# Self products of 4096 rows on one core: which queue loads which part of the input, when, and in what packets

## Chip, cores and metric

One core of one Trainium2 chip. The metric is the device time of one execution in microseconds (us). The kernel before takes 1261.74 us, the median of three runs that lie between 1261.66 and 1261.79.

## What is computed

The input has 4096 rows of 256 float32 values. For each row all products of two of its values are wanted, the upper triangle only, row by row of the triangle: 32,896 products for each input row.

```python
def _L0_rec_ref(inputs):              # inputs: (4096, 256) float32
    dot = jnp.einsum('bi,bj->bij', inputs, inputs)
    iu, ju = jnp.triu_indices(inputs.shape[1])
    return dot[:, iu, ju]             # (4096, 32896) float32
```

The input is 4.19 MB, the output 538.97 MB.

## The kernel before

**Tiles.** Partition p holds the 32 input rows 32p to 32p+31, one after the other, in the tile `xt` (`flat` is the same tile as one long row a partition). Two rows make a *unit*: 512 floats, 2 KB a partition, 256 KB in all partitions. There are 16 units. The output of a unit is cut into three *pieces* of some 10,944 columns (`even_borders`), so there are 48 pieces. A piece is computed into one of two places in SBUF (`places`, `PLACES = 2`) and stored from there by one DMA (`sync`, line 392). A store moves, for each of 128 partitions, two contiguous runs of 43,776 or 44,032 bytes.

**Loop.** A *pass* `h` covers two units, that is six pieces `p` = 0 to 5 (`PASS = 6`). There are eight passes. The loop is rotated: pieces 0 and 1 of pass 0 are computed ahead (`AHEAD = 2`), and each turn of the hardware loop computes pieces 2 to 5 of pass `h` and then 0 and 1 of pass `h+1`. The very first piece is stored in five parts (`FIRST`), so that the first store can go out early; ScalarE (`scalar`) helps VectorE (`vector`) with the two pieces ahead.

**Who computes.** VectorE multiplies a stretch of a row by one broadcast value (line 275), GpSimd does the same for the tail of each piece (line 360). A piece's first VectorE instruction waits until the place is free (semaphore `free`, set by the store that last used it) and lets GpSimd start (`go`); VectorE's last instruction of the piece waits for GpSimd (`g_done`), and then SyncE issues the store (`v_done`).

**How the input comes in.** Three groups of loads:

- `NEAR`, issued by SyncE at the beginning (line 432): unit 0 alone; units 3, 4, 7 and 8 in runs of 4 KB; unit 12. That is six units.
- `EARLY`, issued by GpSimd at the beginning (line 327, called from the loop over `STEPS`): units 1, 2, 5 and 6 in runs of 4 KB. The 128 partitions are taken as a comb: every third partition in each of three DMAs (42 partitions each), and the last two partitions in a fourth.
- `LATE`, issued by GpSimd in pass 2 after piece 2 (`late`, line 327): units 9 to 11 and 13 to 15, in runs of 6 KB, as DMAs of 100, 3 and 25 partitions.

**Marks.** Between these DMAs GpSimd issues small ones (`mark`, line 321) that load two runs of 256 bytes a partition into a tile nobody reads, for a chosen number of partitions (`STEPS` = 5, 2, 2, 12, 4 and `SKIP` = 13).

**What waits for loads.** VectorE and ScalarE wait for unit 0 (`loaded[0]`) before they begin, GpSimd waits for it before its first `EARLY` load. Before the loop, VectorE and GpSimd wait for all `NEAR` loads, for `EARLY` (`far`) and for the marks. GpSimd waits for the `LATE` loads in pass 2 after piece 5.

**Queues.** Loads and stores that SyncE issues follow each other on its queue (q1). GpSimd's are on another queue (q0). Both are served by the same 16 DMA engines.

The first part of the first piece is computed by VectorE at line 236, in instructions that take both rows of the unit at once.

Of the kernel before, what the change touches and what calls it, by code (L numbers as in the profile page):

```python
# [12 lines left out]
P = 128  # L13
UNIT = 64
REPEAT = 2
PIECES = 3
EDGE = 32
NEAR = [(0, 1, 1), (3, 7, 2), (12, 13, 1)]
EARLY = (1, 5, 2)
LATE = (9, 13, 3)  # L20
WHEN = 2
BEGUN, HAD = 2, 5
HELPED = 1
HELP = 18.0
COMB = 3
STEPS = (5, 2, 2, 12, 4)
TENS, ODD, SKIP = 100, 3, 13
MARK = 64
PLACES = 2
SETS = 5  # L30
# [1 line left out]
AHEAD = 2  # L32
# [103 lines left out]
def kernel(  # L136
# [45 lines left out]
    loaded = [semaphore(f"loaded{k}") for k in range(len(NEAR))]  # L182
    far, marked = semaphore("far"), semaphore("marked")
    teeth = P // COMB
    rest = P - COMB * teeth

    def take(engine, sem, value: int):
        engine.wait_ge(sem, value).then_inc(sem, -value)  # L188
# [36 lines left out]
    def vector(h, pieces: range, ahead: bool, done: int = 0, joined: int = 0) -> tuple:  # L225
        for p in pieces:
            place, copied = places[p % PLACES], None
            parts = blocks(p, ahead)
            if ahead and p == 0:
                for c, (_, _, _, block, lo) in enumerate(parts):  # L230
                    if c == DIRECT:
                        nc.vector.tensor_copy(xp, x_of(h, 0)).then_inc(v_own, 1)  # L232
                        done += 1
                        copied = done
                    for i, j, at, length in block:
                        ins = nc.vector.tensor_tensor(  # L236
                            place[:, :, at - lo : at - lo + length],
                            window(x_of(h, 0)[:, j:], [[d, REPEAT], [1, 1], [1, length]]),
                            window(xp[:, i:] if c >= DIRECT else x_of(h, 0)[:, i:], [[d, REPEAT], [1, 1], [0, length]]),
                            ALU.mult,  # L240
                        )
                        if copied:
                            ins._wait_ge(v_own, copied).then_inc(go, 1)
                            copied = None
                    ins.then_inc(v_done, 1)
                continue
            shared = not ahead or p == HELPED
            if ahead and p == HELPED:
                take(nc.vector, x_copied, 1)
            first = None  # L250
            if not ahead and p % PIECES == 0:
                ins = nc.vector.tensor_copy(xv[:, :each], x_of(h, p // PIECES))  # L252
                ins._wait_ge(v_own, done).then_inc(v_done, 1)
                nc.vector.tensor_copy(xp, x_of(h, p // PIECES)).then_inc(v_own, 1)  # L254
                done += 1
                first = (v_own, done)
            if not ahead:
                if use(p) == uses:
                    take(nc.vector, free[p % PLACES], 16 * uses)
                elif first:  # L260
                    nc.vector.wait_ge(free[p % PLACES], 16 * use(p))  # L261
                else:
                    first = (free[p % PLACES], 16 * use(p))
            for _, _, _, block, lo in parts:
                order = interleave(block)
                waits = schedule(order)
                end = len(order) - 1
                if shared and end in waits:
                    waits[end - 1] = waits.pop(end)
                counted = {*waits.values(), *([end] if (p + 1) % PIECES == 0 else [])}  # L270
                number = {k: done + 1 + c for c, k in enumerate(sorted(counted))}
                assert 0 < min(counted, default=end) and end - 1 not in counted | {0}
                for k, ((i, j, at, length), m, _) in enumerate(order):
                    at -= lo
                    ins = nc.vector.tensor_tensor(  # L275
                        place[:, :, at : at + m * length],
                        window(xv[:, j:], [[d, REPEAT], [1, m], [1, length]]),
                        window(xp[:, i:], [[d, REPEAT], [1, m], [0, length]]),
                        ALU.mult,
                    )  # L280
                    if k == 0 and first:
                        ins._wait_ge(*first)
                    elif k == end and shared:
                        joined += 1
                        ins._wait_ge(g_done, joined)
                    elif k in waits:
                        ins._wait_ge(v_own, number[waits[k]])
                    if k in counted:
                        ins.then_inc(v_own, 1)
                    elif k == end:  # L290
                        ins.then_inc(v_done, 1)
                    elif k == 0 and not ahead:
                        ins.then_inc(go, 1)
                done += len(counted)
        return done, joined

    def scalar(pieces: range):

        xa = xt[:, 0, :each]
        for p in pieces:  # L300
            for _, _, block, _, lo in blocks(p, True):
                todo = [
                    nc.scalar.activation(  # L303
                        places[p][:, r, at - lo : at - lo + length],
# [4 lines left out]
                    for i, j, at, length in block  # L309
                    for r in range(REPEAT)  # L310
                ]
                if todo:
                    todo[-1].then_inc(a_done, 1)
                else:
# [5 lines left out]
        of = window(x_in[lo:hi], [[2 * MARK, 2], [1, MARK]])  # L320
        nc.gpsimd.dma_start(marks[lo:hi, :, :MARK], of).then_inc(marked, 16)  # L321

    def load(of_units: tuple, rows: slice):
        one, two, units = of_units
        dims = [[(two - one) * each, 2], [1, units * each]]
        to, of = (window(ap[rows, one * each :], dims) for ap in (flat, x_in))
        nc.gpsimd.dma_start(to, of).then_inc(far, 16)  # L327

    def late(h, p: int):
        with nc.gpsimd.If(h == WHEN):  # L330
            if p == BEGUN:
                load(LATE, slice(0, TENS))
                load(LATE, slice(TENS, TENS + ODD))
                mark(0, SKIP)
                load(LATE, slice(TENS + ODD, P))
            else:
                nc.gpsimd.wait_ge(far, 16 * (COMB + 4))
                nc.gpsimd.wait_ge(marked, 16 * (COMB + 3))
                nc.gpsimd.drain()

    def gpsimd(h, pieces: range, ahead: bool):

        done = turns = 0
# [6 lines left out]
        for p in [HELPED] if ahead else pieces:  # L350
            place = places[p % PLACES]
            block, lo = helped(p) if ahead else next((block, lo) for _, _, block, _, lo in blocks(p, False))
            turns += not ahead
            order = interleave(block)
            waits = schedule(order)
            counted = {*waits.values()}
# [14 lines left out]
                    ins.then_inc(g_own, 1)  # L371
            done += len(counted)
            ins.then_inc(g_done, 1)
            if p in (BEGUN, HAD) and not ahead:
                late(h, p)
        nc.gpsimd.sem_inc(g_own, -done)
        if turns:
            nc.gpsimd.sem_inc(go, -turns)  # L378

    def sync():  # L380
        done = ahead_done = 0
# [13 lines left out]
        for sem, count in ((v_done, done), (a_done, ahead_done)):  # L395
            nc.sync.sem_inc(sem, -count)

    def settle(counts: tuple):
        for sem, count in zip((v_own, g_done), counts):
            nc.vector.sem_inc(sem, -count)  # L400

    def all_pieces(engine, pieces_of):
        by_vector = engine is nc.vector
        counts = pieces_of(0, range(AHEAD), True)
        if by_vector:
            settle(counts)
        for sem in loaded[1:]:
            engine.wait_ge(sem, 16)
        engine.wait_ge(far, 16 * (COMB + 1))
        engine.wait_ge(marked, 16 * (COMB + 2))  # L410
        kind = engine.engine
        with nc.Fori(  # L412
            0,
# [4 lines left out]
            counts = pieces_of(h, range(AHEAD, PASS), False)  # L418
            with engine.If(h < passes - 1):
                nxt = nc.s_assert_within(h + 1, 0, passes - 1)  # L420
                if by_vector:
                    settle(vector(nxt, range(AHEAD), False, *counts))
                else:
                    pieces_of(nxt, range(AHEAD), False)
        if by_vector:
            nc.vector.wait_ge(v_own, counts[0]).then_inc(v_done, 1)
            settle(counts)

    for (one, two, units), sem in zip(NEAR, loaded):
        dims = [[(two - one) * each, 2 if two - one > units else 1], [1, units * each]]  # L430
        to, of = (window(ap[:, one * each :], dims) for ap in (flat, x_in))
        nc.sync.dma_start(to, of).then_inc(sem, 16)
    nc.vector.memset(edge, 0.0).then_inc(warm, 1)  # L433
    take(nc.scalar, warm, 1)
    nc.scalar.activation(edge[:, :1], edge[:, 1:2], AF.Copy, scale=edge[:, 2:3])  # L435
    for engine in (nc.vector, nc.scalar):
        engine.wait_ge(loaded[0], 16)
    at = 0
    for k, step in enumerate(STEPS):
# [44 lines left out]
```

## Time and profile before

| | |
|---|---|
| runs, median (lowest to highest) | 1261.74 us (1261.66 to 1261.79) |
| the profiled execution | 1261.66 us |
| span of its instructions | 1259.9 us |
| VectorE busy | 792.5 us, 63% of the span |
| GpSimd busy | 800.1 us, 64% |
| ScalarE busy | 27.1 us, 2% |
| bytes read / written in HBM | 4.21 MB / 538.97 MB |
| SyncE's loads at the beginning | issued from 0.96 us on, three |
| GpSimd's loads at the beginning | four, from 3.92 us on, with five marks, the last issued at 8.05 us |
| GpSimd's loads in pass 2 | three and a mark, issued from 364.40 to 366.39 us |

Times in the trace are counted from the first instruction of the span. The span leaves out what lies before the first and after the last instruction, here 1.8 us of the execution's time. "Issue to landing" of a DMA counts from the instruction on the issuing engine to the last of its completions, the time in the queue included. A DMA engine works through *packets*: one contiguous run, with its own size and time in the trace.

### The profile page before, as it was taken

How to read it: one execution, taken by the hardware profiler on the slowest of the kernel's cores; microseconds unless marked ns; L12 is line 12 of the kernel's file. 1: busy time of each engine (PE TensorE's matmuls, PEld its weight loads, DVE VectorE, ACT ScalarE, POOL GpSimd, SP SyncE). 2: the span in 40 equal slices, each digit the busy share in tenths (PEclk: the TensorE clock that was granted, in tenths of full speed). 3: DMA queues.
4: the chain of work that ended last, by engine and by line, in shares of the span. 5: the costliest groups of instructions: out<-in, count | busy, mean ns of one | idle time of the engine just before them, and what ended most of it. 6: DMA issues, size and time to landing. Idle time of an engine off the chain costs nothing. (4 is left out here: it accounts for less than half of the span.)

```text
span 1259.9 us, 2787 instructions
## 1 busy us (share of the span) xinstructions
DVE 792.5 (63%) x1256; ACT 27.1 (2%) x74; POOL 800.1 (64%) x1124
## 2 busy tenths in 40 slices
DVE  8656746667475674766647666486655866468560
ACT  8000000000000000000000000000000000000000
POOL 7477674776666766477665775567656676566750
DMA  9999999999999999999999999999999999999999
GB/s 375 441 427 441 429 437 431 434 434 434 436 433 428 435 435 431 435 428 438 430 438 430 439 428 438 430 438 431 434 436 431 437 431 436 429 436 429 440 428 395
DMA packets 15847, 543.25 MB, mean 431 GB/s; under 512 B 1466, under 2 KB 1504, under 8 KB 3296
## 3 DMA queue, kind: packets, MB, share of 16 engines
q1 hardware_dynamic: 14704, 540.54, 99.3%
q0 software_dynamic: 1136, 2.64, 0.6%
q14 instruction: 7, 0.06, 0.0%
HBM read 4.21 MB, written 538.97 MB: 431 GB/s over the span
## 5 line engine op out<-in xcount | busy, mean ns | idle before, releaser
L360 POOL TENSOR_TENSOR o<-xv 128x696 f32<-128x696 f32 (+33 forms) x1105 | 791.1, 756 | 416.8 <-DVE o L275 416.5
L275 DVE TENSOR_TENSOR o<-xv,xp 128x588 f32<-128x588 f32 (+4 forms) x1195 | 761.1, 712 | 430.3 <-DMA out_dram<-o 195.3
L303 ACT ACTIVATE o<-x 128x198 f32<-128x198 f32 (+34 forms) x72 | 25.5, 447 | 0.8 <-DMA x<-in_r_inputs_dram 0.8
L254 DVE COPY xp<-x 128x512 f32 x15 | 10.3, 688 | 0.0
L236 DVE TENSOR_TENSOR o<-x,xp 128x470 f32<-128x470 f32 (+18 forms) x19 | 9.7, 585 | 0.0
L236 DVE TENSOR_TENSOR o<-x 128x510 f32<-128x510 f32 (+9 forms) x10 | 5.7, 646 | 2.5 <-DMA x<-in_r_inputs_dram 2.5
L252 DVE COPY xv<-x 128x512 f32 x15 | 6.4, 427 | 0.5
L327 POOL DMA_DIRECT2D x<-in_r_inputs_dram x7 | 4.5, 649 | 1.6 <-DMA x<-in_r_inputs_dram 1.6
L321 POOL DMA_DIRECT2D marks<-in_r_inputs_dram x6 | 3.6, 602 | 1.2 <-SPq L175 1.2
L346 POOL MEMSET xv<- 128x1 f32 x1 | 0.1, 93 | 2.1 <-POOLq L188 2.1
L435 ACT ACT_TABLE_LOAD x1 | 1.3, 1283 | 1.2 <-ACTq L188 1.2
L433 DVE MEMSET edge<- 128x32 f32 x1 | 0.1, 85 | 1.0 <-SPq L175 1.0
L232 DVE COPY xp<-x 128x512 f32<-128x512 f32 x1 | 0.7, 684 | 0.0
L347 POOL COPY xv<-x 128x512 f32<-128x512 f32 x1 | 0.6, 609 | 0.0
L435 ACT ACTIVATE edge<-edge 128x1 f32<-128x1 f32 x1 | 0.3, 296 | 0.0
L471 POOL MEMSET const-float32-0.0<- 128x1 f32 x1 | 0.1, 98 | 0.2 <-issue 0.2
L471 POOL MEMSET const-bfloat16-1.0<- 128x1 bf16 x1 | 0.1, 101 | 0.0
L471 POOL MEMSET const-uint8-127<- 128x1 uint8 x1 | 0.1, 101 | 0.0
L471 POOL MEMSET const-float32-1.0<- 128x1 f32 x1 | 0.1, 98 | 0.0
## 6 DMA issues: line engine op xcount, KB each, us to landing
out_dram<-o SPq DMA_DIRECT2D x31, 10944.0 KB, 32.9
out_dram<-o SPq DMA_DIRECT2D x16, 11008.0 KB, 31.2
out_dram<-o SPq DMA_DIRECT2D x1, 4352.0 KB, 18.6
out_dram<-o SPq DMA_DIRECT2D x1, 2624.0 KB, 13.8
out_dram<-o SPq DMA_DIRECT2D x1, 1984.0 KB, 11.8
out_dram<-o SPq DMA_DIRECT2D x1, 1280.0 KB, 9.9
x<-in_r_inputs_dram POOLq DMA_DIRECT2D x1, 1200.0 KB, 39.7
x<-in_r_inputs_dram SPq DMA_DIRECT2D x1, 1024.0 KB, 5.2
```

What stands on the lines that cost most here:

```text
L232: nc.vector.tensor_copy(xp, x_of(h, 0)).then_inc(v_own, 1)
L236: ins = nc.vector.tensor_tensor(place[:, :, at - lo : at - lo + length], window(x_of(h, 0)[:, j:], [[d, REPEAT], [1, 1], [1, length]]), wi ...
L252: ins = nc.vector.tensor_copy(xv[:, :each], x_of(h, p // PIECES))
L254: nc.vector.tensor_copy(xp, x_of(h, p // PIECES)).then_inc(v_own, 1)
L275: ins = nc.vector.tensor_tensor(place[:, :, at : at + m * length], window(xv[:, j:], [[d, REPEAT], [1, m], [1, length]]), window(xp[:, i:] ...
L303: nc.scalar.activation(places[p][:, r, at - lo : at - lo + length], xa[:, r * d + j : r * d + j + length], AF.Copy, scale=xa[:, r * d + i ...
L321: nc.gpsimd.dma_start(marks[lo:hi, :, :MARK], of).then_inc(marked, 16)
L327: nc.gpsimd.dma_start(to, of).then_inc(far, 16)
L347: nc.gpsimd.tensor_copy(xv[:, :each], x_of(0, 0)).then_inc(g_own, 1)
L360: ins = nc.gpsimd.tensor_tensor(place[:, :, at : at + m * length], window(xv[:, j:], [[d, REPEAT], [1, m], [1, length]]), window(xv[:, i:] ...
L435: nc.scalar.activation(edge[:, :1], edge[:, 1:2], AF.Copy, scale=edge[:, 2:3])
L471: nc = _bacc.Bacc("TRN2", target_bir_lowering=False, num_devices=1)
```

## The change

SyncE's first load is split into the two rows of unit 0 (two DMAs in runs of 1 KB), and it then loads units 1, 2, 4 and 5 in runs of 4 KB and units 3 and 15 in runs of 2 KB: seven units. GpSimd loads nothing at the beginning; the comb and its marks are gone. In pass 1, ahead of piece 5, it loads units 6, 10 and 14 in runs of 2 KB and units 7 to 9 and 11 to 13 in runs of 6 KB: each group as one DMA of 120 partitions and one of 8, with a mark ahead of each of the four DMAs (5, 2, 7 and 3 partitions). It waits for them in pass 2, ahead of piece 5. The first instruction of the first part is done row by row: on VectorE as two instructions, on ScalarE by sorting the rows, with row 1's waiting for `loaded[1]`. GpSimd waits for both rows before it begins. The wait for `far` and `marked` ahead of the loop is gone. GpSimd's counts are now carried from the loop's pieces 2 to 5 into 0 and 1, as VectorE's were, and subtracted once (`settle`).

```diff
-NEAR = [(0, 1, 1), (3, 7, 2), (12, 13, 1)]
-EARLY = (1, 5, 2)
-LATE = (9, 13, 3)
-WHEN = 2
-BEGUN, HAD = 2, 5
+NEAR = [(1, 2, 3, 2), (3, 2, 12, 1)]
+LATE = [(6, 3, 4, 1), (7, 2, 4, 3)]
+BEGUN, HAD = (1, 5), (2, 5)
-COMB = 3
-STEPS = (5, 2, 2, 12, 4)
-TENS, ODD, SKIP = 100, 3, 13
+MOST = 120
+STEPS = (5, 2, 7, 3)
...
-                    for i, j, at, length in block:
+                    todo = [(run, 0, REPEAT) for run in block]
+                    if c == 0:
+                        todo[:1] = [(block[0], r, 1) for r in range(REPEAT)]
+                    for (i, j, at, length), r, rows in todo:
...
+                        if r:
+                            ins._wait_ge(loaded[r], 16)
...
-    def load(of_units: tuple, rows: slice):
-        one, two, units = of_units
-        dims = [[(two - one) * each, 2], [1, units * each]]
-        to, of = (window(ap[rows, one * each :], dims) for ap in (flat, x_in))
-        nc.gpsimd.dma_start(to, of).then_inc(far, 16)
+    def units(of_units: tuple, rows: slice) -> tuple:
+        one, parts, step, of_part = of_units
+        dims = [[step * each, parts], [1, of_part * each]]
+        return tuple(window(ap[rows, one * each :], dims) for ap in (flat, x_in))

     def late(h, p: int):
-        with nc.gpsimd.If(h == WHEN):
-            if p == BEGUN:
-                load(LATE, slice(0, TENS))
-                load(LATE, slice(TENS, TENS + ODD))
-                mark(0, SKIP)
-                load(LATE, slice(TENS + ODD, P))
-            else:
-                nc.gpsimd.wait_ge(far, 16 * (COMB + 4))
-                nc.gpsimd.wait_ge(marked, 16 * (COMB + 3))
+        if p == BEGUN[1]:
+            with nc.gpsimd.If(h == BEGUN[0]):
+                at = 0
+                todo = [(part, rows) for part in LATE for rows in (slice(0, MOST), slice(MOST, P))]
+                for step, (part, rows) in zip(STEPS, todo):
+                    mark(at, at + step)
+                    at += step
+                    nc.gpsimd.dma_start(*units(part, rows)).then_inc(far, 16)
+        if p == HAD[1]:
+            with nc.gpsimd.If(h == HAD[0]):
+                nc.gpsimd.wait_ge(far, 16 * len(STEPS))
+                nc.gpsimd.wait_ge(marked, 16 * len(STEPS))
                 nc.gpsimd.drain()
...
+            if not ahead:
+                late(h, p)
             order = interleave(block)
...
-            if p in (BEGUN, HAD) and not ahead:
-                late(h, p)
...
-        for sem in loaded[1:]:
+        for sem in loaded[REPEAT:]:
             engine.wait_ge(sem, 16)
-        engine.wait_ge(far, 16 * (COMB + 1))
-        engine.wait_ge(marked, 16 * (COMB + 2))
...
-    for (one, two, units), sem in zip(NEAR, loaded):
-        dims = [[(two - one) * each, 2 if two - one > units else 1], [1, units * each]]
-        to, of = (window(ap[:, one * each :], dims) for ap in (flat, x_in))
-        nc.sync.dma_start(to, of).then_inc(sem, 16)
+    for r in range(REPEAT):
+        part = slice(r * d, (r + 1) * d)
+        nc.sync.dma_start(flat[:, part], x_in[:, part]).then_inc(loaded[r], 16)
+    for part, sem in zip(NEAR, loaded[REPEAT:]):
+        nc.sync.dma_start(*units(part, slice(0, P))).then_inc(sem, 16)
...
-    at = 0
-    for k, step in enumerate(STEPS):
-        if k == 1:
-            nc.gpsimd.wait_ge(loaded[0], 16)
-        if k:
-            load(EARLY, slice(k - 1, k + COMB * (teeth - 1), COMB) if k <= COMB else slice(P - rest, P))
-        mark(at, at + step)
-        at += step
-
+    nc.gpsimd.wait_ge(loaded[0], 16)
+    nc.gpsimd.wait_ge(loaded[1], 16)
```

More of the change, by code (lines that the diff above doesn't have):

```diff
@@ L181 @@
     head, v_done, a_done, go = (semaphore(s) for s in ("head", "v_done", "a_done", "go"))
-    loaded = [semaphore(f"loaded{k}") for k in range(len(NEAR))]
+    loaded = [semaphore(f"loaded{k}") for k in range(REPEAT + len(NEAR))]
     far, marked = semaphore("far"), semaphore("marked")
-    teeth = P // COMB
-    rest = P - COMB * teeth
     def take(engine, sem, value: int):
@@ L234, in vector @@
                         copied = done
-                    for i, j, at, length in block:
+                    todo = [(run, 0, REPEAT) for run in block]
+                    if c == 0:
+                        todo[:1] = [(block[0], r, 1) for r in range(REPEAT)]
+                    for (i, j, at, length), r, rows in todo:
+                        left = xp if c >= DIRECT else x_of(h, 0)
                         ins = nc.vector.tensor_tensor(
-                            place[:, :, at - lo : at - lo + length],
-                            window(x_of(h, 0)[:, j:], [[d, REPEAT], [1, 1], [1, length]]),
-                            window(xp[:, i:] if c >= DIRECT else x_of(h, 0)[:, i:], [[d, REPEAT], [1, 1], [0, length]]),
+                            place[:, r : r + rows, at - lo : at - lo + length],
+                            window(x_of(h, 0)[:, r * d + j :], [[d, rows], [1, 1], [1, length]]),
+                            window(left[:, r * d + i :], [[d, rows], [1, 1], [0, length]]),
                             ALU.mult,
                         )
+                        if r:
+                            ins._wait_ge(loaded[r], 16)
                         if copied:
@@ L300, in scalar @@
         for p in pieces:
-            for _, _, block, _, lo in blocks(p, True):
+            for c, (_, _, block, _, lo) in enumerate(blocks(p, True)):
+                order = [(run, r) for run in block for r in range(REPEAT)]
+                if p == c == 0:
+                    order.sort(key=lambda of: of[1])
                 todo = [
@@ L308, in scalar @@
                     )
-                    for i, j, at, length in block
-                    for r in range(REPEAT)
-                ]
+                    for (i, j, at, length), r in order
+                ]
+                if p == c == 0:
+                    for r in range(1, REPEAT):
+                        todo[[of for _, of in order].index(r)]._wait_ge(loaded[r], 16)
                 if todo:
@@ L321, in mark, with gpsimd @@
         nc.gpsimd.dma_start(marks[lo:hi, :, :MARK], of).then_inc(marked, 16)
-    def load(of_units: tuple, rows: slice):
-        one, two, units = of_units
-        dims = [[(two - one) * each, 2], [1, units * each]]
-        to, of = (window(ap[rows, one * each :], dims) for ap in (flat, x_in))
-        nc.gpsimd.dma_start(to, of).then_inc(far, 16)
-    def late(h, p: int):
-        with nc.gpsimd.If(h == WHEN):
-            if p == BEGUN:
-                load(LATE, slice(0, TENS))
-                load(LATE, slice(TENS, TENS + ODD))
-                mark(0, SKIP)
-                load(LATE, slice(TENS + ODD, P))
-            else:
-                nc.gpsimd.wait_ge(far, 16 * (COMB + 4))
-                nc.gpsimd.wait_ge(marked, 16 * (COMB + 3))
+    def units(of_units: tuple, rows: slice) -> tuple:
+        one, parts, step, of_part = of_units
+        dims = [[step * each, parts], [1, of_part * each]]
+        return tuple(window(ap[rows, one * each :], dims) for ap in (flat, x_in))
+    def late(h, p: int):
+        if p == BEGUN[1]:
[10 more added lines that the diff above has]
+                nc.gpsimd.wait_ge(marked, 16 * len(STEPS))
                 nc.gpsimd.drain()
-    def gpsimd(h, pieces: range, ahead: bool):
-        done = turns = 0
+    def gpsimd(h, pieces: range, ahead: bool, done: int = 0, turns: int = 0) -> tuple:
         if ahead:
@@ L373, in gpsimd @@
             ins.then_inc(g_done, 1)
-            if p in (BEGUN, HAD) and not ahead:
-                late(h, p)
-        nc.gpsimd.sem_inc(g_own, -done)
-        if turns:
-            nc.gpsimd.sem_inc(go, -turns)
+        return done, turns
     def sync():
@@ L396, in sync, with settle @@
             nc.sync.sem_inc(sem, -count)
-    def settle(counts: tuple):
-        for sem, count in zip((v_own, g_done), counts):
-            nc.vector.sem_inc(sem, -count)
+    def settle(engine, counts: tuple):
+        for sem, count in zip((v_own, g_done) if engine is nc.vector else (g_own, go), counts):
+            if count:
+                engine.sem_inc(sem, -count)
     def all_pieces(engine, pieces_of):
[L403 to L406, printed above, removed]
-        for sem in loaded[1:]:
+        settle(engine, pieces_of(0, range(AHEAD), True))
+        for sem in loaded[REPEAT:]:
             engine.wait_ge(sem, 16)
-        engine.wait_ge(far, 16 * (COMB + 1))
-        engine.wait_ge(marked, 16 * (COMB + 2))
         kind = engine.engine
@@ L420, in all_pieces @@
                 nxt = nc.s_assert_within(h + 1, 0, passes - 1)
[L421 to L425, printed above, removed]
-            nc.vector.wait_ge(v_own, counts[0]).then_inc(v_done, 1)
-            settle(counts)
-    for (one, two, units), sem in zip(NEAR, loaded):
-        dims = [[(two - one) * each, 2 if two - one > units else 1], [1, units * each]]
-        to, of = (window(ap[:, one * each :], dims) for ap in (flat, x_in))
-        nc.sync.dma_start(to, of).then_inc(sem, 16)
+                settle(engine, pieces_of(nxt, range(AHEAD), False, *counts))
+        if engine is nc.vector:
+            nc.vector.wait_ge(v_own, counts[0]).then_inc(v_done, 1)
+        settle(engine, counts)
+    for r in range(REPEAT):
[3 more added lines that the diff above has]
+        nc.sync.dma_start(*units(part, slice(0, P))).then_inc(sem, 16)
     nc.vector.memset(edge, 0.0).then_inc(warm, 1)
```

## The prediction

> **What bounds the kernel now.** I read the busy shares first, then the slices and the queues, then the waits, last the beginning in windows.
>
> ```profile
> DVE 792.5 (63%) x1256; ACT 27.1 (2%) x74; POOL 800.1 (64%) x1124
> DMA  9999999999999999999999999999999999999999
> DMA packets 15847, 543.25 MB, mean 431 GB/s; under 512 B 1466, under 2 KB 1504, under 8 KB 3296
> q1 hardware_dynamic: 14704, 540.54, 99.3%
> q0 software_dynamic: 1136, 2.64, 0.6%
> ```
>
> No engine is busy for more than two thirds of the span, and the DMA engines are full in all 40 slices. The stores' queue alone takes 99.3% of 16 engines' time. So the time is the work of the DMA engines, and a wait on VectorE or GpSimd costs something only where it leaves a DMA engine without a packet.
>
> ```profile
> POOL o L360 <- DVE o L275: 416.5, 46, 12.6
> DVE o L275 <- DMA out_dram<-o: 195.3, 31, 9.1
> SPq L392 <- DVE o L275: 739.2, 30, 27.2
> ```
>
> The waits agree: VectorE waits for stores to land, GpSimd waits for VectorE. Both have room in every piece.
>
> ```profile
> 263.72 0.52 DVE L275 TENSOR_TENSOR o<-xv,xp 128x354 f32<-128x354 f32 x1 [3.76 <-POOL o L360]
> 264.27 28.24 SPq L392 DMA_DIRECT2D out_dram<-o  x2
> 271.53 20.11 DVE L275 TENSOR_TENSOR o<-xv,xp 128x260 f32<-128x260 f32 x41 [7.29 <-DMA out_dram<-o]
> 272.04 14.71 POOL L360 TENSOR_TENSOR o<-xv 128x292 f32<-128x292 f32 x39 [8.35 <-DVE o L275]
> ```
>
> This is the place where the change puts its late loads: GpSimd ends piece 4 of pass 1 at 263.69 us and idles 8.35 us before piece 5. In that piece VectorE works 20.11 us and GpSimd 14.71, so GpSimd has another 5.4 us.
>
> ```profile
> 0.00:10.00 10.00, 6.41 (x13) 7.94 (x21) 5.67 (x13) 1.00 0.79 266
> 10.00:20.00 10.00, 10.00 (x20) 10.00 (x29) 8.94 (x9) 1.00 1.03 414
> L327 POOL DMA_DIRECT2D x<-in_r_inputs_dram x7: 569/622/859, 3.9 to 366.4; - x7
> L321 POOL DMA_DIRECT2D marks<-in_r_inputs_dram x6: 564/580/729, 1.6 to 365.8; - x6
> ```
>
> The DMA engines stand idle only in the first 2 us, before the first load arrives (share 0.03 from 0 to 2 us, 0.98 from 2 to 6), and after the last store.
>
> So the span is: 2.0 us to the first packet, then the busiest DMA engine's packets, then 1.3 us from the last landing (1258.59 us) to the end. What counts is not the mean of the 16 but the one that ends last. The completions of the last store show how far apart they are: the first lands at 1256.22, the last at 1258.59, the mean is 1257.97. The busiest is 0.6 us behind the mean. An even spread could gain no more than that.
>
> **The price of a packet.** From the packets' records, start to next start on one engine: 2 KB 80 ns, 4 KB 155 ns, 6 KB 230 ns, 43,776 bytes 1614 ns. A 1 KB packet isn't in the trace. It lies between a 512-byte one (23 ns) and a 2 KB one (80 ns); I take 42 ns, as it lies on the line through the other sizes.
>
> **Loads at the beginning.** A 128-partition load gives each engine 8 partitions. SyncE's six units before: 16 packets of 2 KB and 16 of 4 KB, 1.28 + 2.48 = 3.76 us an engine. After: 16 of 1 KB, 16 of 4 KB, 16 of 2 KB, 0.67 + 2.48 + 1.28 = 4.43 us (4.1 to 5.0 by the bounds for 1 KB). That is +0.67 us for every engine alike.
>
> GpSimd's loads before are not alike. The records of the late loads show ten engines with 20 packets of 6 KB each, which is 100 partitions in tens, one engine with none, and the rest 10 or 12. I read the comb in the same way: 42 partitions on 14 engines, three each, thrice. An engine that has part in all of them has 18 × 155 ns = 2.79 us early and 20 × 230 ns = 4.60 us late, 7.39 us together. The mean over 16 engines is 2.48 + 3.68 = 6.16 us.
>
> After: each partition of the second-pass load costs 3 × 80 + 2 × 230 = 700 ns. I read 120 partitions as 8 on each of 15 engines, 5.60 us, and the 8 partitions left over as one on each of eight engines, 240 ns and 460 ns, at most 0.70 us together. So most engines have 5.6 to 6.3 us, one has next to none. The mean is 5.60 us.
>
> On the mean nothing happens: 3.76 + 6.16 = 9.92 us before, 4.43 + 5.60 = 10.03 after. The completion packets of thirteen small DMAs become those of eight, worth some -0.07 us. For an engine that was and stays in the heaviest group: +0.67 + 6.30 - 7.39 = -0.42 us.
>
> **But the uneven load has a counterpart.** Some engines lose time to other things, which I find by following each engine's packets. One is slowed by about 0.12 us a store throughout, some 5.5 us in all, and this is the one with no late packets. Two others are held up by instruction loads of 8 KB (queue 14; seven inside the span, gaps of 0.30 us and longer packets behind them): between the stores 3 and 9 one falls behind by about 2.1 us, the other by about 1.0. The first of these had nothing of the comb and only five partitions late, 2.3 us. After the change it has 5.60 us like the others. So its end moves: before, the heaviest at 7.39; after, 0.67 + 5.60 + 2.1 = 8.37 us, which is +1.0 us. The engine that is slowed by 5.5 us has 0.67 + 5.5 = 6.2 us if it is the one that 120 partitions leave out. As the first mark has five partitions before and after, I take it that the same one is left out.
>
> **The beginning without GpSimd's loads.** Before, two engines had none of the comb, and so show what a queue of SyncE alone does there: they stand idle for some 0.4 us ahead of the first store's packets (issued at 4.83, first packet at 7.21 us) and 0.6 us ahead of the second store's (issued at 6.69, first packet at 9.56). The comb covered this on the other 14. After, the loads last 0.67 us longer, which covers the first gap, and the first store can go out a little earlier: the first row's load is half as large, VectorE has one instruction more (0.69 us become two of some 0.38). From below, nothing is lost; from above, 1.0 us is, on all engines. I take 0.3, since the loads cover one of the gaps and the other shrinks with the earlier start.
>
> **GpSimd's issues.** In pass 1 it issues four loads and four marks: 4 × 0.62 + 4 × 0.58 = 4.8 us. They lie in the idle 8.35 us and wait behind nothing; SyncE's stores are on another queue. VectorE waits for GpSimd only at the end of the piece, so there is cover of 8.35 + 5.4 us. Were the cover gone, a late store would cost nothing until the DMA engines' lead is used up: the store of that piece was issued at 292.13 us, and the previous one landed from 295.5 to 297.3, so 2.5 us more. The loads themselves have time: 40 turns an engine at one load packet for each store packet, as the records of the late loads show it (1.85 us a turn with 6 KB), are some 72 us, until about 345; GpSimd waits for them only ahead of piece 5 of pass 2, at about 430.
>
> The Trainium skill speaks against this place. "SBUF — State Buffer", section "A bandwidth-pool intuition that's wrong (but worth ruling out)", says that a DMA issued by GpSimd took about 3100 ns instead of 620 beside a copy on VectorE, as descriptors can't be written while VectorE holds the shared port. By it eight issues would take 24.8 us, the store would be 8.5 us late, and the time some 1271. The row shows 569 to 859 ns for loads issued at 3.9 to 7.5 us with VectorE busy, and 0.62 is the median; I go by the row.
>
> **The waits added.** VectorE's second instruction waits for row 1, issued 0.45 us behind row 0; behind it waits the rest of the first part, and SyncE's first store. This is in the 0.3 us above. The removed wait ahead of the loop was over by 15.8 us, long before VectorE's 38.6; nothing is gained there.
>
> **Sum.** -0.07 + 1.0 + 0.3 = +1.2 us on the span of 1259.9: 1261.1. The profiled execution took 1261.66 and the median is 1261.74, so 1.8 us lie around the span: 1262.9, say 1262.8. A measurement of this kernel can't tell less than about 0.2%, 2.5 us, from no change, and this is less.
>
> **The rivals.**
> - *Even, or a little better* (12%): if the 2.1 us fall away or lie elsewhere, only -0.42 - 0.07 + 0.3 = -0.2 us is left: 1261.5. For it: a changed program may load its instructions at other moments. Against: queue 14 is served anyway. To be faster by 2.5 us is out of reach: an even spread is worth 0.6 us and the mean is unchanged. I leave 3% for it.
> - *The lost time meets the load* (17%, the other side): the 120 partitions leave out another engine than the one that is slowed by 5.5 us. Then this one has 0.67 + 5.60 + 5.5 = 11.8 us against 7.39: +4.4, 1266. If only the instruction loads are dearer, 3.1 instead of 2.1 us, and fall on an engine with 6.30: 0.67 + 6.30 + 3.1 - 7.39 = +2.7, 1264.4. It decides as soon as one engine's own share and loss exceed 9.2 us (7.39 + 2.5 - 0.67). For it: the comb left out two engines, the change only one. Against: the first mark is the same.
> - *GpSimd is stopped in its issues* (5%): each engine gets some 40 load packets at once where the trace shows 20 to 23. If a queue takes no more, GpSimd waits until the first load has drained, 24 turns of 1.7 us = 41 us; less 8.35 + 5.4 + 2.5 of cover, 24 us are lost: 1286. Nothing in the profile shows such a limit.
>
> The forecast has 63%, with a range of its own of 1261.6 to 1264.2. For all cases: 1260.6 (the even case without a gap) to 1265.8 (nearly the slowed engine in full). Slower by over 0.2%: 15% of the second rival, 5% of the third, 3% of the forecast, 23%. Faster 3%, the rest within.
>
> **What would show it.** The slices stay at 9. The loads at the beginning are on SyncE's queue alone and q0 holds some 2.4 MB, near 264 to 345 us. GpSimd's eight issues take 0.6 us each and end by 270; VectorE's next piece starts as it does now. No gap over 1 us in DMA from 2 us on. The last store's completions are spread wider than 2.4 us, with one or two stragglers. I am wrong if a store in pass 1 or 2 is issued late, if DMA runs dry between 6 and 12 us for more than 1 us, or if one engine ends over 3 us behind the mean.

## The result and the profile after

| | before | after |
|---|---|---|
| median of 10 runs each (lowest to highest) | 1261.76 us (1261.54 to 1262.02) | 1264.74 us (1264.1 to 1266.13) |
| the profiled execution, its span | 1261.66, 1259.9 us | 1264.94, 1263.1 us |
| mean of the last store's 16 completions | 1257.97 us | 1258.36 us |
| the last of them | 1258.59 us | 1261.47 us |

The ratio is 1.0024, with a 95% interval from 1.0014 to 1.0034: the change costs 3.0 us. The forecast was +1.2 us, 1262.8; the time lies inside its range for all cases, 1260.6 to 1265.8, but above the 1261.6 to 1264.2 that it gave to the forecast itself.

First the page after: busy time, the slices, the packets and the two queues.

```profile
DVE 792.6 (63%) x1257; ACT 27.1 (2%) x74; POOL 797.1 (63%) x1119
DMA  9999999999999999999999999999999999999998
GB/s 372 438 436 431 439 429 440 427 436 430 429 434 433 434 433 434 433 433 434 434 433 436 434 437 430 437 431 437 430 439 428 436 431 435 432 435 435 432 433 354
DMA packets 15688, 543.24 MB, mean 430 GB/s; under 512 B 1131, under 2 KB 1404, under 8 KB 3136
q1 hardware_dynamic: 14976, 540.81, 99.2%
q0 software_dynamic: 704, 2.37, 0.5%
```

Hardly anything on the engines has changed, and the DMA engines are full from the first slice to the last but one. The last slice shows the loss: 354 GB/s, where before has 395:

```profile
GB/s 375 441 427 441 429 437 431 434 434 434 436 433 428 435 435 431 435 428 438 430 438 430 439 428 438 430 438 431 434 436 431 437 431 436 429 436 429 440 428 395
```

A slice is 31.5 us, so before it held 12.4 MB and after 11.2 MB. The missing 1.26 MB at 434 GB/s are 2.9 us, nearly the whole difference. The first slice fell from 375 to 372 GB/s, 0.2 us. So nearly nothing shows where the loads were moved away from, and nothing where they were moved to. The time shows at the end, where one DMA engine works while others have finished.

The waits (engine and line, what it waits for: us in total, times, longest) answer to those shown of before.

```profile
POOL o L368 <- DVE o L276: 417.1, 46, 14.0
DVE o L276 <- DMA out_dram<-o: 193.4, 31, 7.5
```

The same two waits, 31 times as before. No wait for a late load has come in.

The timeline around the eight issues (start, us, engine, line, operation, and in brackets the idle time before and what ended it):

```profile
254.72 7.75 POOL L368 TENSOR_TENSOR o<-xv 128x628 f32<-128x628 f32 x9
262.41 0.75 POOL L327 DMA_DIRECT2D marks<-in_r_inputs_dram  x1
263.06 28.40 SPq L396 DMA_DIRECT2D out_dram<-o  x2
...
267.03 0.57 POOL L342 DMA_DIRECT2D x<-in_r_inputs_dram  x1
270.49 20.11 DVE L276 TENSOR_TENSOR o<-xv,xp 128x260 f32<-128x260 f32 x41 [7.46 <-DMA out_dram<-o]
271.00 14.71 POOL L368 TENSOR_TENSOR o<-xv 128x292 f32<-128x292 f32 x39 [3.40 <-DVE o L276]
```

GpSimd issues from 262.41 to 267.60 us, all in its idle time: what was 8.35 us of idle time is now 5.2 us of issues and 3.40 us of idle time. The store in between goes out at 263.06 us, and the next piece begins when its place is free.

The beginning in two windows (busy time of VectorE, ScalarE and GpSimd, clock, DMA share, GB/s):

```profile
0.00:10.00 10.00, 6.88 (x14) 8.41 (x23) 0.20 (x4) 1.00 0.76 238
10.00:20.00 10.00, 10.00 (x20) 10.00 (x29) 9.35 (x9) 1.00 1.03 431
```

The DMA share of the first 10 us is 0.76 against 0.79, worth 0.3 us, and then it is full.

What the views cannot show is which DMA engine ends last. For that I read the records of the stores' completions. Each line gives the 16 completions of the last store, in us before the last one:

```
before  -2.4 -1.3 -1.3 -1.3 -0.6 -0.5 -0.5 -0.5 -0.4 -0.3 -0.3 -0.2 -0.2 -0.1  0.0  0.0
after   -4.2 -4.2 -4.2 -4.1 -3.8 -3.5 -3.4 -3.4 -3.4 -3.4 -3.2 -2.8 -2.1 -2.1 -1.9  0.0
```

The mean moved by +0.4 us, the last completion by +2.9 us. The engine that ends 1.9 us behind all others is the *slow engine*: the one that the prediction found 0.12 us slower in each store. The next, at -1.9, is the *hit engine*: the one to which the prediction gave 2.1 us of lost time by instruction loads (two more end 0.2 us before it). It is taken for that engine by the instruction load that falls on it at 138.2 us, at 139.7 in before. It ends 1.3 to 1.5 us behind most of the engines with the heavier late load; the forecast was 8.37 - 6.97 = 1.4. Were the slow engine no later than it, the span would be about 1261.2 us, which is the forecast's 1261.1. The error is therefore in the slow engine, which the forecast had at 6.2 us and out of the way.

Does the slow engine carry late loads after all? Here are store packets of it and of an ordinary engine while the 6 KB group is loaded, from about 298 to 322 us of the run after, in order (H is a store packet, here of 44,032 bytes, 6 a load packet of 6 KB; +n means that the packet took n ns longer than the usual 1627):

```
ordinary  H 6 H 6 H 6 H 6 H 6 H 6 H 6 H 6 H 6 H 6 H 6 H 6 H
slow      H+41 H+188 H+228 H+215 H+225 H+220 H+212 H+222 H+220 H+213 H+215 H+268 H+213
```

(The records name no engine. I link each packet to the one that starts where it ends, and where two engines start a packet at one moment the link can go wrong. What identifies the slow engine here is that this stretch has no load packet, and that its place among the completions before and after fits.)

It is left out, as forecast. Yet while the others alternate a store packet with a 6 KB packet (1627 + 234 = 1861 ns a turn), its own store packets take some 1843 ns, nearly the same pace, with no load packet between them. The stretches of this row add up to 2.7 us, and with the three packets behind it to 3.5, nearly the 3.7 that the 6 KB group costs a loading engine. So it gained next to nothing from the 6 KB group. In the 2 KB group before it, it ran free, with many of its packets 14 to 31 ns longer. The completions of two stores (counted from 0), one ahead of the late loads and one behind them, again in us before the last of the 16:

```
store 13  -2.6 -2.5 -2.5 -2.4 -2.4 -2.4 -2.3 -2.3 -2.2 -2.2 -2.2 -1.8 -0.9 -0.8 -0.6  0.0
store 17  -2.3 -2.3 -2.3 -2.2 -2.2 -1.8 -1.6 -1.5 -1.5 -1.5 -1.5 -1.2 -0.9 -0.2 -0.2  0.0
```

The slow engine, which falls back by some 0.12 us from store to store, is at -0.9 in the first row and -2.3 in the second: 1.4 us, and 0.5 us of its own drift over four stores, so 1.9 us kept out of 5.60 us that the others carried. The remaining 34 stores at 0.12 us, 4.2 us, put it from 2.3 ahead to 1.9 behind.

### The profile page after: what moved, and what is told of

Read it like the earlier page. It is cut to its first block, busy times and chain, and to the rows that moved or that the text cites. A ratio compares the mean times of both kernels' runs of the same rounds, so it can differ in the third digit from the quotient of the medians.

```text
span 1263.1 us, 2771 instructions
## 1 busy us (share of the span) xinstructions
DVE 792.6 (63%) x1257; ACT 27.1 (2%) x74; POOL 797.1 (63%) x1119
## 5 line engine op out<-in xcount | busy, mean ns | idle before, releaser
L235 DVE TENSOR_TENSOR o<-x 128x255 f32<-128x255 f32 (+9 forms) x11 | 5.8, 602 | 2.1 <-DMA x<-in_r_inputs_dram 2.1
## 6 DMA issues: line engine op xcount, KB each, us to landing
out_dram<-o SPq DMA_DIRECT2D x1, 1984.0 KB, 11.2
```

The lines of the kernel that those rows point to most:

```text
L235: ins = nc.vector.tensor_tensor(place[:, r : r + rows, at - lo : at - lo + length], window(x_of(h, 0)[:, r * d + j :], [[d, rows], [1, 1], ...
```

## The experiments

Four theories, by the names that the expectations use:

- **Paced**, in the later runs **Held**: an engine without load packets runs free only until it is some 2.5 to 4 us ahead of the last one; then its store packets stretch to the pace of the loading ones. The relief of the slow engine comes in one burst, and most of it is lost.
- **Not left out**: the slow engine still has late load packets (the prediction's second rival).
- **Beginning**: the time is lost at the beginning, where GpSimd's comb is gone and the loads no longer balance the engines.
- **Issues**: GpSimd is delayed by what it issues. The timeline above has settled this one.

Each ratio is against the kernel before on the same chip (median 1261.84, 1262.13 and 1261.84 us for the e, f and g runs). "Slow engine behind" is how far it ends behind the next one in the profiled run.

| run | median us | ratio, 95% interval | slow engine behind |
|---|---|---|---|
| after | 1264.74 | 1.0024 [1.0014, 1.0034] | 1.9 |
| e1_all_alike | 1266.55 | 1.0037 [1.0023, 1.0051] | 3.7 |
| e2_next_engine_out | 1266.73 | 1.0039 [1.0024, 1.0053] | 3.8 |
| e3_first_group_alike | 1264.15 | 1.0017 [1.0007, 1.0027] | 1.1 |
| e4_tens | 1266.86 | 1.0041 [1.0027, 1.0055] | 3.8 |
| f1_old_beginning | 1262.07 | 1.0000 [0.9990, 1.0010] | 0.4 |
| f2_two_steps | 1267.35 | 1.0041 [1.0027, 1.0055] | 3.9 |
| f4_nines | 1262.46 | 1.0003 [0.9993, 1.0013] | not last (by 0.2) |
| f5_two_out | 1264.80 | 1.0022 [1.0013, 1.0032] | 1.9 |
| g1_two_steps_two_runs | 1263.13 | 1.0009 [0.9999, 1.0019] | 0.6 |
| g2_before_alike | 1264.30 | 1.0019 [1.0010, 1.0029] | 3.0 |
| g3_second_group_alike | 1265.85 | 1.0032 [1.0020, 1.0043] | 2.1 |

### Take the relief away, move it, halve it

**e1_all_alike**: both late groups as one DMA of 128 partitions each, no marks, so no engine is left out.

```diff
-                todo = [(part, rows) for part in LATE for rows in (slice(0, MOST), slice(MOST, P))]
-                for step, (part, rows) in zip(STEPS, todo):
-                    mark(at, at + step)
-                    at += step
-                    nc.gpsimd.dma_start(*units(part, rows)).then_inc(far, 16)
+                for part in LATE:
+                    nc.gpsimd.dma_start(*units(part, slice(0, P))).then_inc(far, 16)
...
```

> Each group of late loads is one DMA of 128 partitions, without marks: all 16 engines carry 5.6 us. Three theories of the changed kernel's 1264.7 us. 'Paced': the slowed engine (some 0.12 us a store) is the one left out of the late loads, but its own store packets grew longer while the others loaded, so it kept some 2.0 of its 5.6 us; given the load like the others, it ends 2.0 us later: 1266.7 (1266.2 to 1267.4). 'Not left out': that engine has carried the load all along: 1264.7. 'Beginning': the time is lost before 12 us, by one engine's late start of 1.4 us: 1264.7, with the last completion due to that engine.

Measured 1266.55. The relief that the change gives to the slow engine is worth 1.8 us, so it is left out, and the relief works only in part. The queues and slices of e1's page:

```profile
DMA  9999999999999999999999999999999999999997
DMA packets 15464, 543.23 MB, mean 430 GB/s; under 512 B 928, under 2 KB 1184, under 8 KB 2912
q0 software_dynamic: 480, 2.36, 0.4%
```

The bytes are after's, with 224 packets fewer on q0 (the cuts and their marks), and yet the last slice falls to 7: what the time hangs on is who carries the packets, not how many there are. At the end 14 engines stand level, some 4.4 us ahead of the slow one.

**e2_next_engine_out**: the first mark has six partitions instead of five.

```diff
-STEPS = (5, 2, 7, 3)
+STEPS = (6, 2, 7, 3)
```

> The first mark has six partitions instead of five, so that the late loads leave out the next engine. 'Paced': the slowed engine now has the full load, 1266.7 to 1267.4, and the engine left out, which is not slow by itself, shows whether its store packets also grow longer when it is ahead. 'Not left out': 1264.7, or some 1261 to 1262 if the slowed engine is the next one. 'Beginning': 1264.7.

Measured 1266.73, as in e1: with a mark of five it is the slow engine that is left out, and with six it is another. That other engine is not slow by itself, so its packets show the hold alone. It runs free for six or seven packets of the 2 KB group; then four of its packets stretch by 137 to 158 ns, and in the 6 KB group most of them by 172 to 186 ns. At store 17 it is 3.6 us ahead of the last. Together, e1 and e2 refute **Not left out**.

**e3_first_group_alike** leaves the slow engine out of the 6 KB group alone, **g3_second_group_alike** out of the 2 KB group alone.

```diff
+                nc.gpsimd.dma_start(*units(LATE[0], slice(0, P))).then_inc(far, 16)
...
-                todo = [(part, rows) for part in LATE for rows in (slice(0, MOST), slice(MOST, P))]
-                for step, (part, rows) in zip(STEPS, todo):
+                for step, rows in zip(STEPS, (slice(0, MOST), slice(MOST, P))):
...
-                    nc.gpsimd.dma_start(*units(part, rows)).then_inc(far, 16)
+                    nc.gpsimd.dma_start(*units(LATE[1], rows)).then_inc(far, 16)
...
```

(This is e3. g3 cuts `LATE[0]` into 120 and 8 partitions and then loads `LATE[1]` as one DMA of 128.)

> The 2 KB group is one DMA of 128 partitions; only the 6 KB group leaves an engine out. 'Paced', with a lead that is capped at some 2.5 us over the slowest engine: the slowed engine comes to the 6 KB group 1.9 us further back, so it may gain that much before it is held: the time stays at 1264.7 (1264.2 to 1265.3), and only some half as many store packets are long. 'Paced', with a price on each 6 KB packet of the others whatever the lead: 1.9 us more, 1266.6. 'Not left out' and 'Beginning': 1264.7, with as many long packets as before.

> The changed kernel, leaving the engine out of the 2 KB group alone; the 6 KB group, 3.7 us for each engine, is one DMA of 128 partitions. 'Held': in the changed kernel the engine gained its lead in the first group and was held through the second, so nothing is lost: 1264.7 (1264.2 to 1265.3). If what it is spared counts in full, or in half: 1268.4 or 1266.5.

e3 takes 1264.15 us, 0.6 less than after with a third of the relief removed (the two intervals overlap): about the 1264.2 that a capped lead allows, and far from the 1266.6 of a price on each 6 KB packet. There the slow engine has gained nothing from the 2 KB group when the 6 KB group begins. It runs free for six or seven packets, is held for five (+193 to +211 ns), and stands 3.0 us ahead at store 17 instead of 2.3. g3 is a miss for **Held**, which gave 1264.2 to 1265.3: it takes 1265.85, and is 0.70 us better than e1, where the group weighs 1.9 us. In its 2 KB group one packet is stretched by 471 ns, so 1.4 us are kept. The profiled execution, at 1265.29, is the fastest of the seven; what the others lose beyond that, the trace can't say. Against e1 the reliefs are thus worth: 2 KB group alone 0.70, 6 KB group alone 2.40, both 1.81 us. They do not add up. Relief in both groups buys no more than relief in the 6 KB group alone.

### Other cuts

**e4_tens**: both groups in 100, 3 and 25 partitions, as the late loads were before.

```diff
-MOST = 120
-STEPS = (5, 2, 7, 3)
+CUTS = (0, 100, 103, 128)
+STEPS = (5, 0, 13, 1, 0, 13)
...
```

> Both late groups are cut as the kernel before cut its one: 100, 3 and 25 partitions, so ten engines carry 7.0 us, one nothing, five 3.5 to 4.2; the beginning stays as changed. 'Paced': the slowed engine can lead the heavier engines by its cap, so it ends some 1 to 2 us earlier: 1262.3 to 1263.7. 'Not left out': 1264.7 or more. 'Beginning': the engine that starts 1.4 us late ends as late as now or 0.7 us later: 1264.7 to 1265.4.

A miss: 1266.86. The page gives the time from issue to landing of GpSimd's loads (KB each, us):

```profile
x<-in_r_inputs_dram POOLq DMA_DIRECT2D x1, 1200.0 KB, 84.3
x<-in_r_inputs_dram POOLq DMA_DIRECT2D x1, 600.0 KB, 32.8
x<-in_r_inputs_dram POOLq DMA_DIRECT2D x1, 300.0 KB, 113.9
x<-in_r_inputs_dram POOLq DMA_DIRECT2D x1, 150.0 KB, 53.7
x<-in_r_inputs_dram POOLq DMA_DIRECT2D x1, 36.0 KB, 93.6
x<-in_r_inputs_dram POOLq DMA_DIRECT2D x1, 18.0 KB, 36.6
```

They land in the order of issue, 600, 18, 150, 1200, 36, 300 KB, although the 25 partitions lie mostly on other engines than the 100. So the groups of engines load one after another, and in each phase those that do not load are slowed to the pace of those that do (most packets +115 to +130 ns). All pay for all phases. At store 17 the mean of the completions is 378.84 us against 378.03 in after, and the slow engine comes out with a lead of some 0.5 us.

**f5_two_out** cuts 126 and 2 partitions, which leaves two engines out.

```diff
-MOST = 120
-STEPS = (5, 2, 7, 3)
+MOST = 126
+STEPS = (5, 2, 14, 2)
```

> The changed kernel with each late group cut into 126 and 2 partitions instead of 120 and 8: two neighbouring engines are left out, among them the slowed one and (if I have the engines right) the one that instruction loads put last; the others carry 6.3 us. 'Held', with a lead that counts from the last engine: this is now one of the loaded ones, some 2 us earlier than before, and the slowed engine may be further ahead of the rest when the late loads end: 1261.6 to 1263.0. 'Beginning': 1264.7.

A miss in the time: 1264.80, no other than after. That is the figure which **Beginning** gave, but not for its reason. The last engine is again the slow one, 1.9 us behind the next; it is 2.2 us ahead at store 17, hardly less than in after. An engine more left out does not loosen the hold.

### The old beginning with other late loads

These three keep the kernel before and change only the late loads of its pass 2.

**f1_old_beginning**: 120 and 8 partitions; **f4_nines**: 126 and 2; **g2_before_alike**: all 128 at once, so that no engine is left out late.

```diff
-                load(LATE, slice(0, TENS))
-                load(LATE, slice(TENS, TENS + ODD))
-                mark(0, SKIP)
-                load(LATE, slice(TENS + ODD, P))
+                load(LATE, slice(0, P))
...
```

(This is g2. With the values put in, f1 has `load(LATE, slice(0, 120))`, `mark(0, 2)`, `load(LATE, slice(120, P))` in this place, f4 `load(LATE, slice(0, 126))` and `load(LATE, slice(126, P))`.)

> The kernel before, with its loads at the beginning, but its late loads (six units, in pass 2) cut into 120 and 8 partitions instead of 100, 3 and 25. 'Held': an engine without late loads gains some 2.5 to 3.7 us on the last one and is then held to the pace of those that load; the slowed engine had nothing of the comb, comes to the late loads ahead already, is held early, and falls behind by 4 us in the 34 stores that follow: 1262.3 to 1263.2. 'Beginning', which puts the whole loss into what happens before 12 us: 1261.8, as before.

> The kernel before with its late loads cut into 126 and 2 partitions: 14 engines carry 9 partitions, the two that the comb leaves out carry one each. If the last engine is one of the ten that carried 7.4 us, it carries 6.9 now: 1261.2 to 1261.6. If the slowed engine is then the last one, it stays at 1261.8.

> The kernel before with its late loads as one DMA of 128 partitions. The slowed engine then has 3.7 us where it had none; of these it kept some 2 in the kernel with 120 and 8 partitions. 'Held': it is some 2.0 us ahead at store 16, stays there, loses 4.2 us by the end, and ends 2 us behind the next: 1263.8 to 1264.6. 'Beginning': the beginning is that of before, 1261.8.

g2 decides between the theories. The beginning is that of the kernel before, byte for byte, and the time is 1264.30: with the late relief gone, the slow engine ends 3.0 us behind the next. So **Beginning** falls as the whole cause; 2.5 us hang on the late relief of one engine. f1 lies between the two expectations: 1262.07, with the slow engine last by 0.4 us. Beside after it suggests that the beginning has a part all the same: with the late loads cut into the same 120 and 8 partitions, but with the comb in place and six late units instead of nine, nothing is lost. The comb's relief alone was not enough (g2), nor that of the late loads in one burst (after). f4 missed: 1262.46 where 1261.2 to 1261.6 was expected. Its last engine is neither one of the ten heavy ones nor the hit engine, but, as its instruction load at 135.00 us shows, the other one that the prediction found held up by such loads. It is 1.0 us behind the rest, the slow engine apart, from store 13 to the end; making the late load lighter for the ten heavy ones gains nothing.

### The relief in two steps

If a lead can be gained only up to a limit, and the slow engine uses it up at 0.12 us a store, two loads far apart should leave it more. **f2_two_steps** loads units 6 to 9 in pass 1 and 10 to 14 in pass 3, as one run a partition; **g1_two_steps_two_runs** units 6, 7, 9 and 10, then 11, 12, 14 and 15, as two runs a partition, with units 3, 8 and 13 at the beginning.

```diff
-LATE = [(6, 3, 4, 1), (7, 2, 4, 3)]
+LATE = [(6, 1, 4, 4), (10, 1, 5, 5)]
...
-        if p == BEGUN[1]:
-            with nc.gpsimd.If(h == BEGUN[0]):
...
+        if p != 5:
+            return
+        for n, part in enumerate(LATE):
+            with nc.gpsimd.If(h == 2 * n + 1):
...
-        if p == HAD[1]:
-            with nc.gpsimd.If(h == HAD[0]):
...
+            with nc.gpsimd.If(h == 2 * n + 2):
...
```

(f2. g1 has `NEAR = [(1, 2, 3, 2), (3, 3, 5, 1)]` and `LATE = [(6, 2, 3, 2), (11, 2, 3, 2)]`.)

> The changed kernel with its nine late units in two steps: units 6 to 9 in pass 1, units 10 to 14 in pass 3, each as 120 and 8 partitions with the same engine left out. 'Held': between the steps the slowed engine uses up some 1.5 us of its lead, so less of the second step is lost: 1262.4 to 1263.3. 'Beginning': as changed, 1264.7. If the lead is not what matters but the number of load packets beside which it works: 1264.7 too.

> The late units of the changed kernel in two steps, again as 120 and 8 partitions, but with two runs a partition (units 6, 7, 9, 10 in pass 1, units 11, 12, 14, 15 in pass 3; unit 3, 8 and 13 with SyncE's loads), as with one run a partition another engine was left out. 'Held': the slowed engine comes some 1.6 us ahead out of the first step, uses 1.5 us of it up, and gains as much again in the second: 1262.9 to 1263.6. If only the number of load packets counts, or the beginning: 1264.7.

f2 missed, 1267.35, for a reason that is no part of either theory: with one run a partition the same marks leave out another engine. In its trace the slow engine's store packets alternate with load packets of 8 KB, and a different engine is 3.8 us ahead at store 17. The Trainium skill, "DMA: Bandwidth & Descriptors", section "Why a DMA increments its semaphore by 16 and not by 1", gives a rule that would explain this: a DMA takes the largest number of engines up to 16 that divides its slowest dimension; for GpSimd's DMAs a number under 16 is taken in turn from a cursor; and some direct copies of GpSimd depart from this and spread over all 16 with the partitions divided by 16 and rounded up on each, so that 100 partitions lie on engines 0 to 14. By it, 120 partitions use 15 engines and a mark of five moves the cursor by five; that the left-out engine changed with a mark of six in e2 agrees. The copies with one run a partition would be the exception. No run here reads the engines' numbers, so the exception itself is not shown.

g1 has the same two steps with two runs a partition: 1263.13, as **Held** gave it. The slow engine is last by only 0.6 us, and the time is 1.6 us less than after. In two steps the relief is worth 3.4 us against e1, in one burst 1.8 (g1 loads some other units at the beginning, so this comparison is not quite clean).

## Why the prediction was nearly right

- **What bounds the kernel**: right. All slices are full, and what counts is the DMA engine that ends last; +0.4 us on the mean became +3.0 us on the time.
- **The first term, -0.07 us, and the beginning, +0.3 us**: right in sum. The mean of the last completions moved by +0.39 us. By parts they were less good. The loads of SyncE ran slower than priced: 2 KB packets took 132 ns on the mean and 4 KB packets 206, where single ones take 84 and 159 late in the run (SyncE's loads in before: 104 and 177). The last load landed at 8.8 to 9.2 us on 15 engines and at 10.6 on one, and the DMA engines had two short dips instead of two gaps (10.1 of 16 busy from 3.0 to 3.5 us, some 14.5 from 6.5 to 8.0).
- **The hit engine, +1.0 us**: right in size. It ends 1.3 to 1.5 us behind the heavy ones, where 1.4 was worked out. It got there in another way. In the profiled run it is 1.4 us behind already at the first store (by as much as the last load landed late on one engine), and one instruction load at 138 us adds 0.66 us; the forecast had put all 2.1 us between stores 3 and 9. That the two sums agree is luck.
- **The slow engine, "0.67 + 5.5 = 6.2 us if it is the one that 120 partitions leave out"**: here the prediction failed. The condition was true (e1, e2), and the sum was not. It assumed that an engine without late packets keeps the whole 5.60 us that the others lose. It kept 1.9 us, about what the 2 KB group weighs. So the term is 0.67 + 5.5 + (5.60 - 1.9) = 9.9 us, which is more than the 8.37 us of the hit engine, and by the prediction's sum, as 9.9 - 7.39 - 0.07 + 0.3, the change costs 2.7 us; 3.0 was measured. Without the 0.67 it is 9.2 us, just the point from which, in the prediction, its second rival decides. The rival came about in part, and by another way than the one written down.
- **That rival's price**, 11.8 us for a slow engine with the whole late load, so 1266: e1 is this case, and took 1266.55.
- **What before's trace had to say of it**: part of the evidence was there. In before, the slow engine comes out of the late loads 4.4 us ahead of the last one (store 18), and its last packets before that are stretched, four of them by 107 to 170 ns, 0.6 us with the smaller ones. So it was held there too, but only towards the end, and kept about 4 of the 4.60 us that the ten heaviest engines carried. It also had the comb behind it: two engines lead by 3.0 and 2.7 us at store 1. With these two separate reliefs the slow engine is among the last at the end, but not behind them. The change took the first away and asked the second, larger one to do the work of both. The prediction read the number of packets on each engine, and not how far the engine without them came ahead.
- **GpSimd's issues**: right. They take 567 to 805 ns each, 5.2 us together, where 4.8 was worked out, beside VectorE's last instruction of the piece and in idle time. The 3100 ns that the Trainium skill gives for an issue beside a copy on VectorE ("SBUF — State Buffer", "A bandwidth-pool intuition that's wrong (but worth ruling out)") do not show here either; but no issue of GpSimd stood beside a copy, in before as little as here, and only the first mark here began just ahead of a product of VectorE and ran beside it, for 0.75 us:

```profile
L342 POOL DMA_DIRECT2D x<-in_r_inputs_dram x4: 567/668/805, 263.2 to 267.0; - x4
L327 POOL DMA_DIRECT2D marks<-in_r_inputs_dram x4: 570/590/751, 262.4 to 266.4; - x4
```

- **GpSimd stopped in its issues**: did not happen; 704 packets on q0 were taken without a wait. The wait in pass 2 was over at once.
- **What would show it wrong**: "if one engine ends over 3 us behind the mean". It ends 3.1 us behind. This sign fired, and it led to the cause.

What stays open is why an engine without load packets is slowed at all, and what sets the 2.5 to 4 us after which it begins: in after the slow engine was held at once in the 6 KB group, in before only towards its end, and g3 and f5 missed what **Held** gave. The runs show that it happens, to an engine that is slow (after, e3) and to one that is not (e2), and that it follows the loading engines' turn. No run varied the size of the store's packets or the number of stores in flight, which might tell what limits it.

## What to carry to other kernels

When all DMA engines are full, follow the one that ends last, not the mean: here a change that left the mean within 0.4 us cost 3.0. Leaving a slow engine out of a load is worth something, but here its lead was limited to a few microseconds at a time; spread such relief over several loads that lie far apart, as the kernel before did with its comb and its late loads. Which engine a DMA leaves out hangs on its partitions, its pattern and the DMAs before it, so read it off the packets after each edit instead of carrying it over.

## What the runs showed of the hardware

- **An engine without load packets was slowed to the others' pace**: some 1843 ns a store packet of 44,032 bytes instead of 1627, against a turn of 1861 ns on the loading engines (after).
- **A lead seems to have a second limit.** In e1, e2, e4, f2 and g2 the leading engines stand level at 4.4 to 4.5 us ahead of the last, and come no further. I take this for the two places, since a store can't be issued before the last engine has freed one; no run changed the number of places.
- **GpSimd's DMAs were worked one after another**, over all engines: e4's landings above.
- **2 KB runs of GpSimd's DMAs travelled in pairs.** After's 2 KB group should be 384 packets of 2 KB; the trace has 188 of 4096 bytes and 8 of 2048. A pair takes 159 ns, and two packets of 2 KB would take 168.
- **One DMA engine is slower than the rest all the time**, by 0.12 us a store of 25.9 us, in every profiled run. That it is the same engine in all runs is taken from its place, as the records name none.
- **The start of one engine varies with the same beginning**: at the first store the last engine is behind the next by 1.4 us in after, 0.1 in e1, 0.4 in e3 and 0.8 in e4. Each is one execution, so this may differ from execution to execution and not only between programs.
